# Moving output tiles and two value slots around the turn from self- to cross-attention, and padding the context keys with zeros

## The chip, the cores and the metric

The kernel runs on one core of a Trainium2 chip. The metric is the device time of one execution in microseconds. It is given as the median of several executions. One more execution was taken with the profiler, and all durations of single instructions come from that one.

## What is computed

The reference is one transformer block in float32 on `x` of shape 2 x 1024 x 256 and a context of shape 2 x 154 x 192. There are 16 heads of 64 channels.

```python
h = layernorm(x, ln1);  x = attention(h, h, sa_w*) + x        # 1024 keys
h = layernorm(x, ln2);  x = attention(h, context, ca_w*) + x  # 154 keys
h = layernorm(x, ln3);  p = h @ ff_w1 + ff_b1
a, gate = split(p);     x = (a * gelu(gate)) @ ff_w2 + ff_b2 + x

# attention: softmax(q k^T / 8) v for each head, joined, @ wo + bo
```

## The kernel before

Two heads make a pair, so each of the two batch entries has 8 pairs. A pair of one batch entry is a unit, and there are 16 units in self-attention and again 16 in cross-attention. The order of the instructions on every engine is the order in which the program emits them: the schedule is written by hand, in loops over slots, and tile pools add the waits.

**Self-attention** runs in 128 slots, 8 to a unit. A slot takes two groups of 64 query rows. TensorE makes the scores (L379), DVE takes the maximum of each row (L539), ACT the exponentials with their sums (L390). The keys of one query row lie in two halves on different partitions, so a small DMA on the SP queue exchanges the row statistics `st` (L400). A slot later `join` (L404 to L417) makes the common scale: on POOL `dd` (L408 to L410), on ACT `ee` (L412), on POOL `zz` and `den` (L414, L416). DVE takes the reciprocal `rd` (L486) and POOL multiplies the probabilities by it (L490, four instructions in a slot). Two slots after its scores a group is transposed by DVE into `pT` (L504). When the four slots of a half unit are transposed, two value slots multiply them with the values on TensorE (`self_values`, `weigh`, L426) and ACT copies the sums to `oT` (L524).

In the slots that have no values of their own, `run_work` fills TensorE from lists. `work` holds the projections of the next unit, `outs` the output tiles (L357: four matmuls for one tile of 128 rows; DVE adds the result to `x`, L364), and `side` the pieces of a normalization. `later` holds work that is issued one piece in each slot, among it the bias additions on POOL (L259) and DMAs. The result of a piece is copied out of PSUM in the slot after, by `flush(stores)` or `flush(adds)`. Pieces from `run_work` share two PSUM banks (`mm_tile`), scores share two tiles of two banks each (`ps_s`), and value sums have two banks (`sum_tile`). A piece can start only when the bank of the piece but one before it has been copied out.

**Cross-attention** runs in 48 slots, three to a unit. A slot makes the scores of three, three or two query tiles (L654), DVE the maximum `neg` (L659), ACT the exponentials (L670), POOL scales by the reciprocals one slot later (L681), and DVE transposes two slots later into a ring (`pT_ca`, L697). SP's DMAs regroup blocks of the ring into the tile `wf` (L714), and four or more slots later `cross_values` (L730) uses them. The context values `v_ca` have 154 rows: two copies of ACT bring the first 128 of them to their place (L627), one the last 26 (L628). The last block of 128 x 256 is first set to zero by POOL (L613), and DMAs then spread its rows over the partitions (L630, L635).

The tile `wf` also holds the weights of the feed-forward part, which are loaded from `hold_gated` on, two DMAs in a slot. It takes the buffer of the last self-attention `pT`, so it has to wait for the last value slot.

**The turn between the two** is where the change lies. The last unit has slots 120 to 127 (`p`), and cross slots are counted from 0 (`c`). In the last unit before the change, slots 120, 121, 124 and 125 run one piece each: the two query projections of the first cross unit, its keys, its values. The last four output tiles of the first half of batch entry 1 (tiles 4 to 7) enter `outs` in cross slot 0. The last two value slots run in cross slots 2 and 3, inside `self_drain`, that is ahead of the projections that `run_work` puts into these slots.

Of the kernel before, what the change touches and what calls it, by code (L numbers as in the profile page):

```python
# [8 lines left out]
F32 = mybir.dt.float32  # L9
# [4 lines left out]
P = 128  # L14
# [4 lines left out]
def tile_transformer_block(ctx: ExitStack, tc: tile.TileContext, a: dict, out: bass.AP):  # L19
    nc = tc.nc  # L20
# [3 lines left out]
    B, S, D = x.shape  # L24
# [6 lines left out]
    NT = S // P  # L31
# [7 lines left out]
    VC = 2 * P  # L39
    HB = 512  # L40
    QG = 2 * KB
    NM = P // QG
    QH = S // 2
    GH = QH // QG
# [104 lines left out]
    ident = const.tile([P, P], F32, tag="ident", name="ident")  # L149
    make_identity(nc, ident)  # L150

    ctxT = const.tile([CC, 2, B * T], F32, tag="ctxT", name="ctxT")

    def turn_rows():
        pt = spare["bank"]("p_rows")
# [5 lines left out]
    def turn_context(b):  # L161
        pc = spare["bank"](f"pc{b}")
        for c in range(2):
            for i in range(2):
                nc.tensor.transpose(
                    pc[:CC, c * T + i * KP:c * T + (i + 1) * KP],
                    cn[b][:, i, c * CC:(c + 1) * CC], ident[:KP, :KP],
                )
        return lambda: nc.scalar.copy(
            ctxT[:, :, b * T:(b + 1) * T], pc[:CC, :2 * T].rearrange("p (c k) -> p c k", c=2)  # L170
        )

    hT, vs, qk, oT = {}, {}, {}, {}
# [265 lines left out]
    def run(piece):  # L439
        done = piece()  # L440
        if done is not None:
            (adds if getattr(done, "adds", False) else stores).append(done)
# [109 lines left out]
    def self_beside(ui):  # L552

        if ui + 2 >= NU:
            load_pair("ca", ui + 2 - NU)
        elif ui > 0:
            load_pair("sa", units[ui + 2][1])
        nxt = self_pieces(*units[ui + 1]) if ui + 1 < NU else cross_pieces(*units[0])
        if ui + 1 < NU:
            work.extend(nxt)  # L560
        else:

            work.extend(nxt[:2])
            held.extend(nxt[2:])
        if HP <= ui < NU - 2:
            ob, oh = divmod((ui - HP) // HP, 2)
            t0 = (ui % HP) * 2
            out_pieces("sa", ob, oh, (t0, t0 + 1))
        if ui == 1:
            norm_beside("sa", 1)  # L570
        if ui == NPAIR + HP:
            norm_beside("ca", 0)

    def self_drain(p):

        late = scale_groups(*joins.pop(0)) if joins else None
        if p - LAG < SA:
            turn_groups(p - LAG)
        if late:
            late()  # L580
        h, hg = divmod(p, SH)
        if hg >= LAG and h - 1 < 2 * NU:
            run(lambda: self_values(h - 1, hg - LAG))


    CG = [(t, min(TG, NT - t)) for t in range(0, NT, TG)]
# [3 lines left out]
    def cross_pieces(b, pr):  # L590

        t = {}

        def q(n):
            if n == 0:
                t["q"] = p2.tile([P, S], F32, tag="QT", name=f"q_ca{b}_{pr}")
                t["k"] = p2.tile([P, S], F32, tag="KT", name=f"k_ca{b}_{pr}")
                qk["ca", b, pr] = (t["q"], t["k"])
            return project_half(t["q"], f"q_ca{b}_{pr}", wsl["ca", pr, "q"], hT["ca", b], n, scale)

        def keys():
            pk = mm_tile(f"pk_ca{b}_{pr}")
            for c in range(2):
                nc.tensor.matmul(
                    pk[:, :T], lhsT=wsl["ca", pr, "k"][:, c, :],
                    rhs=ctxT[:, c, b * T:(b + 1) * T], start=(c == 0), stop=(c == 1),
                )
            return lambda: nc.scalar.copy(t["k"][:, :T], pk[:, :T])

        def values():  # L610

            v = vs["ca", b, pr // 2] = pt_.tile([P, NM + 1, VC], F32, tag="V", name=f"v_ca{b}_{pr}")
            nc.gpsimd.memset(v[:, NM, :], 0.0)  # L613
            pv = mm_tile(f"pv_ca{b}_{pr}")
            m = T - P
            for n, rows_ in ((0, P), (1, m)):
                for c in range(2):
                    nc.tensor.matmul(
                        pv[:rows_, n * VC:(n + 1) * VC],
                        lhsT=ctxT[:, c, b * T + n * P:b * T + n * P + rows_],  # L620
                        rhs=wsl["ca", pr, "v"][:, c, :], start=(c == 0), stop=(c == 1),
                    )

            def store():
                for n in range(NM):
                    own = slice(n * QG, (n + 1) * QG)
                    nc.scalar.copy(v[own, n, :], pv[own, :VC])  # L627
                nc.scalar.copy(v[:m, NM, :], pv[:m, VC:])  # L628
                later.insert(0, lambda: [
                    nc.sync.dma_start(  # L630
                        out=v[(1 - n) * QG:(2 - n) * QG, n, :], in_=v[n * QG:(n + 1) * QG, n, :])
                    for n in range(NM)
                ])
                later.insert(1, lambda: [
                    nc.sync.dma_start(out=v[a4 * KB:a4 * KB + m, NM, :], in_=v[:m, NM, :])  # L635
                    for a4 in range(1, P // KB)
                ])

            return store

        return [lambda: q(0), lambda: q(1), keys] + ([values] if pr % 2 == 0 else [])

    def cross_first(c):

        ui, n = divmod(c, len(CG))
        b, pr = units[ui]
        t0, nt = CG[n]
        q, k = qk["ca", b, pr]
        k = k[:, :T]
        sc = ps_s.tile([P, 2, HB], F32, tag="s", name=f"sc_{c}")  # L650
        for i in range(nt):
            for j in range(2):
                r = slice(j * DH, (j + 1) * DH)
                nc.tensor.matmul(  # L654
                    sc[:, j, i * T:(i + 1) * T], lhsT=q[r, (t0 + i) * P:(t0 + i + 1) * P],
                    rhs=k[r, :], start=True, stop=True,
                )
        neg = small.tile([P, 2, TG], F32, tag="neg", name=f"neg_{c}")
        nc.vector.tensor_reduce(  # L659
            neg[:, :, :nt], sc[:, :, :nt * T].rearrange("p j (i k) -> p j i k", k=T), AX.X, ALU.max,  # L660
            negate=True,
        )

        def then():
            pr_ = pp_.tile([P, 2, TG, NB * KB], F32, tag="P", name=f"p_{c}")
            nc.gpsimd.memset(pr_[:, :, :, T:], 0.0)
            den = small.tile([P, 2, TG], F32, tag="den", name=f"den_{c}")
            for j in range(2):
                for i in range(nt):
                    nc.scalar.activation(  # L670
                        pr_[:, j, i, :T], sc[:, j, i * T:(i + 1) * T], AF.Exp,
                        bias=neg[:, j, i:i + 1], accum_out=den[:, j, i:i + 1],
                    )

            def late():

                rden = small.tile([P, 2, TG], F32, tag="rden", name=f"rden_{c}")
                nc.vector.reciprocal(rden[:, :, :nt], den[:, :, :nt])  # L678
                for j in range(2):
                    for i in range(nt):  # L680
                        nc.gpsimd.tensor_scalar(  # L681
                            pr_[:, j, i, :T], pr_[:, j, i, :T], rden[:, j, i:i + 1], 1.0,
                            op0=ALU.mult, op1=ALU.mult,
                        )
                crossed[c] = pr_

            return late

        return then
# [172 lines left out]
    with tc.manual_schedule():  # L862
# [45 lines left out]
        for p in range(SA):  # L908
            if p % (2 * SH) == 0:
                self_beside(p // (2 * SH))  # L910
            if p == SA - SH:
                work.extend(held)
                held.clear()
            then = self_first(p)
            flush(stores)
            late = then()
            if p >= LAG:
                turn_groups(p - LAG)
            flush(adds)
            if late:  # L920
                late()
            if later:
                later.pop(0)()
            h, hg = divmod(p, SH)
            if h == 0 or hg < LAG:

                full = hg % 2 == 0 or outs and p < SA - 2 * SH
                run_work(2 if full and p < SA - 2 * SH else 1, 1, sum_tile)
            else:
                run(lambda: self_values(h - 1, hg - LAG))  # L930

        for c in range(CA):
            if c == 0:
# [1 line left out]
                    [P, 2 * NK, QH // 2], F32, tag="pT", name="pT_ca"  # L935
                ).rearrange("p a b -> p (a b)")[:, :3 * 2 * NB * NT * KB].rearrange(
                    "p (u n j q) -> p u n j q", u=3, n=NB, j=2)
            if c == 0:
                out_pieces("sa", B - 1, 0, range(NT // 2, NT))
            if c == SH + 1:  # L940
                out_pieces("sa", B - 1, 1, range(NT))
                outs.append(lambda: load_out("ca"))
            if c == SH:
                w1, w2 = hold_gated()
            if c % len(CG) == 0:
                cross_beside(c // len(CG))
# [12 lines left out]
            cross_weigh(c)  # L959
            flush(stores)  # L960
            run_work(2, 1, n_sum=2 * (SH < c < 2 * NPAIR and c % len(CG) == 0))
            for _ in range(min(2, len(later))):
                later.pop(0)()

# [58 lines left out]
```

## Time and profile before

| | us |
|---|---|
| median of 3 runs | 1173.76 (1172.14 to 1174.32) |
| profiled execution, its own time | 1171.99 |
| span of the profiled execution | 1170.1 |
| TensorE busy | 1142.5 |
| DVE busy | 830.1 |
| POOL busy | 667.5 |
| ACT busy | 644.1 |

The span goes from the first to the last instruction. The profile names every group by its line, its engine and the tiles it writes and reads. "Idle before" is the time that the engine stood still just ahead of an instruction, with the instruction that ended the wait. `PEld` are weight loads, which overlap with matmuls. Each float32 matmul of the program appears as two records. `po` is a value slot, `s` the self scores, `sc` the cross scores, `pq`, `pk` and `pv` projections, `py` an output tile, `poc` the cross values.

Self-attention takes the time to 729.5 us, cross-attention the time to about 1000 us, and the feed-forward part the rest.

### The profile page before, as it was taken

What the parts mean: (1) busy time and instruction counts of PE and PEld (TensorE: products, weight loads), DVE (VectorE), ACT (ScalarE), POOL (GpSimd) and SP (SyncE); (2) the same over time, 40 slices, a digit from 0 to 9 for tenths busy, and PEclk for the clock granted to TensorE, in tenths of its full rate; (3) what the DMA queues carried; (4) which work ended last, traced back from release to release, by engine and by line L of the source; (5) the groups of instructions that cost most, each with busy time, mean ns of one, the idle gap of its engine ahead of it and who ended that gap; (6) DMA issues with size and microseconds to landing.
All of it is one profiled execution on the core that took longest, in us unless ns stands there. A gap on an engine that the chain in (4) does not pass through costs nothing.

```text
span 1170.1 us, 31736 instructions
## 1 busy us (share of the span) xinstructions
PE 1142.5 (98%) x11931; PEld 672.0 (57%) x11931; DVE 830.1 (71%) x1170; ACT 644.1 (55%) x2055; POOL 667.5 (57%) x1563
## 2 busy tenths in 40 slices
PE   9999999999999999999999998999999999999998
PEld 6434444545545545545545443665556567888887
DVE  4888998898888898898989887547555664232222
ACT  5656676665666666566666755447655572041111
POOL 1778777877767777777777787436644453030000
PEclk9999999999999999999999998999999999999999
DMA  2411011101101101101101100166444433000000
GB/s 82 109 26 34 12 25 34 21 21 34 21 16 34 21 16 34 21 16 34 21 16 21 27 20 7 52 167 157 111 103 99 102 80 73 1 19 10 18 10 18
DMA packets 87018, 51.06 MB, mean 44 GB/s; under 512 B 30742, under 2 KB 77650, under 8 KB 86866
## 3 DMA queue, kind: packets, MB, share of 16 engines
q1 hardware_dynamic: 83650, 46.42, 17.6%
q10 hardware_dynamic: 3216, 2.62, 0.7%
q8 instruction: 94, 1.54, 0.5%
q14 instruction: 58, 0.48, 0.1%
HBM read 19.52 MB, written 2.10 MB: 18 GB/s over the span
## 4 chain that ended last, share of the span: by engine, by line
PE 78%; ACT 7%; POOL 6%; DVE 3%; issue 3%; DMA 2%; SPq 1%; DVEq 0%; ACTq 0%; POOLq 0%
PE po L426 15%; PE s L379 15%; PE pa L818 9%; PE py_sa L357 5%; PE py_ca L357 5%; PE pf L841 5%; ACT p L390 4%; PE pq_ca L296 4%; PE poc L730 4%; PE pv_sa L312 4%; PE pk_sa L296 3%; POOL p L490 3%; PE pq_sa L296 3%; PE sc L654 3%; DMA st<-st 2%
## 5 line engine op out<-in xcount | busy, mean ns | idle before, releaser
L390 ACT ACTIVATE p<-s,st 128x512 f32<-128x512 f32 x512 | 345.1, 686 | 218.7 <-DVE st L539 207.8
L490 POOL TENSOR_SCALAR p<-p,rd,ee 128x512 f32<-128x512 f32 x512 | 385.6, 767 | 43.9 <-DVE rd L486 43.3
L539 DVE TENSOR_REDUCE st<-s 128x2 f32<-128x1024 f32 x256 | 301.4, 1219 | 44.8 <-PE s L379 36.9
L504 DVE STREAM_TRANSPOSE pT<-p 128x1024 f32<-128x1024 f32 x256 | 302.4, 1219 | 0.5 <-POOL p L490 0.4
L379 PE MATMUL s<-k_sa,q_sa 64*32 64x512 f32 x4096 | 256.7, 601 | 19.1 <-ACT p L390 18.0
L426 PE MATMUL po<-pT,v_sa 64*64 64x256 f32 x4096 | 236.1, 380 | 1.2 <-DVE pT L504 1.2
L426 PEld LDWEIGHTS po<-pT,v_sa 64*64 64x64 f32 x4096 | 150.8, 133 | 110.4 <-issue 39.4
L681 POOL TENSOR_SCALAR p<-p,rden 128x154 f32<-128x154 f32 x256 | 96.8, 398 | 119.8 <-DVE rden L678 118.6
L379 PEld LDWEIGHTS s<-k_sa,q_sa 64*32 64x32 f32 x4096 | 59.6, 106 | 151.5 <-ACT p L390 64.2
L670 ACT ACTIVATE p<-sc,neg 128x154 f32<-128x154 f32 x256 | 96.0, 394 | 88.6 <-DVE rden L678 84.4
L818 PE MATMUL pa<-hT_ln,wf 128*128 128x256 f32 x512 | 121.0, 379 | 0.0
L827 DVE SCALAR_TENSOR_TENSOR u<-pa,cols,gate 128x256 f32<-128x256 f32 x64 | 31.0, 484 | 124.1 <-ACT gate L824 124.1
L824 ACT ACTIVATE gate<-pa,cols 128x256 f32<-128x256 f32 x64 | 30.3, 474 | 152.1 <-PE pa L818 152.1
L818 PEld LDWEIGHTS pa<-hT_ln,wf 128*128 128x128 f32 x512 | 96.8, 190 | 13.7 <-issue 0.8
L390 ACT ACTIVATION_READ_ACCUMULATOR p<-s,st 128x1 f32 x512 | 103.6, 202 | 0.0
L659 DVE TENSOR_REDUCE neg<-sc 128x6 f32<-128x924 f32 (+1 forms) x48 | 48.6, 1013 | 48.4 <-PE sc L654 48.4
L414 POOL TENSOR_TENSOR zz<-ee,st 128x8 f32<-128x8 f32 x128 | 25.9, 202 | 81.6 <-ACT ee L412 81.6
L312 PEld LDWEIGHTS pv_sa<-sa_wv,hT_ln 128*128 128x128 f32 x512 | 59.3, 192 | 16.3 <-issue 13.8
L841 PE MATMUL pf<-wf,u 128*128 128x256 f32 x256 | 65.0, 379 | 0.2 <-DVE u L827 0.2
L312 PE MATMUL pv_sa<-sa_wv,hT_ln 128*128 128x128 f32 x512 | 62.4, 278 | 0.0
L296 PE MATMUL pk_sa<-hT_ln,sa_wk 128*128 128x512 f32 (+1 forms) x132 | 60.8, 596 | 0.2 <-ACT q_sa L305 0.2
L357 PE MATMUL py_ca<-ca_wo,o_ca 128*128 128x256 f32 x256 | 60.8, 384 | 0.3 <-ACT hT_ln L238 0.3
(73 smaller groups left out, 1230.1 us busy)
## 6 DMA issues: line engine op xcount, KB each, us to landing
wf<-pT_ca SPq DMA_DIRECT2D x128, 128.0 KB
st<-st SPq DMA_DIRECT2D x512, 1.0 KB
v_sa<-v_sa SPq DMA_DIRECT2D x64, 128.0 KB
wf<-in_L_xattn_ff_w_dram SPq DMA_DIRECT2D x12, 256.0 KB
sa_wq<-in_L_xattn_sa_wq_dram SPq DMA_DIRECT2D x16, 128.0 KB
sa_wk<-in_L_xattn_sa_wk_dram SPq DMA_DIRECT2D x16, 128.0 KB
sa_wv<-in_L_xattn_sa_wv_dram SPq DMA_DIRECT2D x16, 128.0 KB
ca_wq<-in_L_xattn_ca_wq_dram SPq DMA_DIRECT2D x16, 128.0 KB
```

The costliest lines, as they stand in the source:

```text
L296: nc.tensor.matmul(pq[:, own], lhsT=wt[:, c, :], rhs=h[:, c, n * HB + own.start:n * HB + own.stop], start=(c == 0), stop=(c == NC - 1),)
L312: nc.tensor.matmul(pv[:, i * P:(i + 1) * P], lhsT=h[:, c, (n * GT + i) * P:(n * GT + i + 1) * P], rhs=wt[:, c, :], start=(c == 0), stop=(c ...
L357: nc.tensor.matmul(py[:, :D], lhsT=o[:, i, t * P:(t + 1) * P], rhs=wo[kind][:, half * HP + i, :], start=(i == 0), stop=(i == HP - 1),)
L379: nc.tensor.matmul(sc[a4 * KB:(a4 + 1) * KB, j, :], lhsT=q[r, c:c + KB], rhs=k[r, h * HB:(h + 1) * HB], start=True, stop=True, tile_positi ...
L390: nc.scalar.activation(pr[:, j, :], sc[:, j, :], AF.Exp, bias=st[:, 0, 0, i, j:j + 1], accum_out=st[:, 0, 1, i, j:j + 1],)
L426: nc.tensor.matmul(po[a2][j * DH:(j + 1) * DH, :QH // 2], lhsT=v[r, t, e, j * DH:(j + 1) * DH], rhs=pT[r, j * NK + n, :], start=(t == 0 an ...
L490: nc.gpsimd.tensor_scalar(pr[:, j, :], pr[:, j, :], rd[:, c:c + 1], ee[:, 0, c:c + 1], op0=ALU.mult, op1=ALU.mult,)
L504: nc.vector.transpose(halves[h][:, :, c:c + KB], groups.pop(0).rearrange("p j (n k) -> p (j n) k", k=KB))
L539: nc.vector.tensor_reduce(st[:, 0, 0, i, :], sc[i], AX.X, ALU.max, negate=True)
L681: nc.gpsimd.tensor_scalar(pr_[:, j, i, :T], pr_[:, j, i, :T], rden[:, j, i:i + 1], 1.0, op0=ALU.mult, op1=ALU.mult,)
L818: nc.tensor.matmul(pa[:, half, :TF * P], lhsT=w1[:, c, half * DF + f * P:half * DF + (f + 1) * P], rhs=h[:, c, t0 * P:(t0 + TF) * P], star ...
L841: nc.tensor.matmul(sums[blk][i][:, :D], lhsT=sums[blk, "u"][:, f, i * P:(i + 1) * P], rhs=w2[:, f, :], start=(f == 0), stop=(f == NF - 1),)
```

## The change

- In the last unit of self-attention, slots 120, 121, 124 and 125 run two pieces each instead of one. The four output tiles that were queued in cross slot 0 are put into the lists of this unit: two behind the query projections, two behind keys and context values.
- The last two value slots move from cross slots 2 and 3 to cross slots 3 and 4, and in each slot behind `run_work`. `hold_gated` moves from cross slot 4 to cross slot 5 with them.
- The transposed context `ctxT` is padded from 154 to 160 columns for each batch entry and set to zero once, at the start, on POOL. The last block of context values is then made from 32 rows, six of them zero, and the eight memsets of `v_ca` are gone.
- The tile `neg` takes the shape 128 x 2 x 4 and shares the buffers of `zz`.

```diff
-    ctxT = const.tile([CC, 2, B * T], F32, tag="ctxT", name="ctxT")
+    ctxT = const.tile([CC, 2, B * TP], F32, tag="ctxT", name="ctxT")
+    nc.gpsimd.memset(ctxT, 0.0)
...
-            work.extend(nxt[:2])
-            held.extend(nxt[2:])
+            spare["out"] = mm_tile
+            last = [lambda t=t: out_piece("sa", B - 1, 0, t) for t in range(NT // 2, NT)]
+            work.extend(nxt[:2] + last[:2])
+            held.extend(nxt[2:] + last[2:])
...
-        h, hg = divmod(p, SH)
-        if hg >= LAG and h - 1 < 2 * NU:
-            run(lambda: self_values(h - 1, hg - LAG))
...
-            nc.gpsimd.memset(v[:, NM, :], 0.0)
-            m = T - P
-            for n, rows_ in ((0, P), (1, m)):
+            for n, rows_ in ((0, P), (1, KB)):
...
-                nc.scalar.copy(v[:m, NM, :], pv[:m, VC:])
+                nc.scalar.copy(v[:KB, NM, :], pv[:KB, VC:])
...
-        neg = small.tile([P, 2, TG], F32, tag="neg", name=f"neg_{c}")
+        neg = small.tile([P, 2, 4], F32, tag="zz", name=f"neg_{c}")
...
-                full = hg % 2 == 0 or outs and p < SA - 2 * SH
-                run_work(2 if full and p < SA - 2 * SH else 1, 1, sum_tile)
+                full = hg % 2 == 0 or outs or p >= SA - 2 * SH
+                run_work(2 if full else 1, 1, sum_tile)
...
-            if c == 0:
-                out_pieces("sa", B - 1, 0, range(NT // 2, NT))
...
-            if c == SH:
+            if c == SH + 1:
                 w1, w2 = hold_gated()
...
             run_work(2, 1, n_sum=2 * (SH < c < 2 * NPAIR and c % len(CG) == 0))
+            if SH - LAG < c <= SH:
+                run(lambda: self_values(2 * NU - 1, c - SH + LAG - 1))
```

More of the change, by code (lines that the diff above doesn't have):

```diff
@@ L41, in tile_transformer_block @@
     QG = 2 * KB
+    TP = NB * KB
     NM = P // QG
@@ L169, in turn_context @@
         return lambda: nc.scalar.copy(
-            ctxT[:, :, b * T:(b + 1) * T], pc[:CC, :2 * T].rearrange("p (c k) -> p c k", c=2)
+            ctxT[:, :, b * TP:b * TP + T], pc[:CC, :2 * T].rearrange("p (c k) -> p c k", c=2)
         )
@@ L605, in keys @@
                     pk[:, :T], lhsT=wsl["ca", pr, "k"][:, c, :],
-                    rhs=ctxT[:, c, b * T:(b + 1) * T], start=(c == 0), stop=(c == 1),
+                    rhs=ctxT[:, c, b * TP:b * TP + T], start=(c == 0), stop=(c == 1),
                 )
@@ L619, in values @@
                         pv[:rows_, n * VC:(n + 1) * VC],
-                        lhsT=ctxT[:, c, b * T + n * P:b * T + n * P + rows_],
+                        lhsT=ctxT[:, c, b * TP + n * P:b * TP + n * P + rows_],
                         rhs=wsl["ca", pr, "v"][:, c, :], start=(c == 0), stop=(c == 1),
@@ L634, in store @@
                 later.insert(1, lambda: [
-                    nc.sync.dma_start(out=v[a4 * KB:a4 * KB + m, NM, :], in_=v[:m, NM, :])
+                    nc.sync.dma_start(out=v[a4 * KB:(a4 + 1) * KB, NM, :], in_=v[:KB, NM, :])
                     for a4 in range(1, P // KB)
```

## The prediction

> **What bounds the kernel now.** I read the page first, then busy time by stretch around the place of the change, then the order of time of TensorE, ACT and POOL there, and last the chain of waits of the first 20 us.
>
> ```profile
> span 1170.1 us, 31736 instructions
> ...
> PE 1142.5 (98%) x11931; PEld 672.0 (57%) x11931; DVE 830.1 (71%) x1170; ACT 644.1 (55%) x2055; POOL 667.5 (57%) x1563
> ...
> PEclk9999999999999999999999998999999999999999
> ```
>
> TensorE is the bound, and the change removes no work from it. It can win only time in which TensorE waits, or runs slowly: the one 8 in the clock row covers 702 to 731 us, the last unit of self-attention.
>
> ```profile
> 682.43:706.13 23.70, 21.85 (x304) 8.63 (x300) 20.38 (x23) 14.24 (x43) 19.73 (x44) 1.00 0.06 12
> 706.13:712.50 6.37, 4.08 (x34) 1.17 (x35) 5.70 (x7) 3.27 (x11) 5.56 (x12) 0.74 0.04 5
> ...
> 719.95:726.20 6.25, 3.87 (x41) 0.89 (x44) 3.08 (x5) 3.47 (x11) 3.18 (x10) 0.73 0.02 3
> ...
> 739.48:758.41 18.93, 18.93 (x189) 13.11 (x189) 7.25 (x15) 6.87 (x30) 5.83 (x19) 1.00 0.09 30
> ```
>
> Columns: length, then busy time of PE, PEld, DVE, ACT, POOL, then the granted clock. Two stretches of 6 us have TensorE a third idle and at three quarters of its clock; from 739.48 on it never waits.
>
> ```profile
> 705.34 0.79 PE L604 MATMUL pk_ca<-ctxT,ca_wk 96*128 96x154 f32 x4
> 708.42 3.30 PE L379 MATMUL s<-k_sa,q_sa 64*32 64x512 f32 x32 [2.29 <-ACT p L390]
> 711.65 2.53 PE L618 MATMUL pv_ca<-ca_wv,ctxT 96*128 96x256 f32 x8
> ...
> 716.27 3.68 PE L426 MATMUL po<-pT,v_sa 64*64 64x256 f32 x64
> 722.33 3.31 PE L379 MATMUL s<-k_sa,q_sa 64*32 64x512 f32 x32 [2.38 <-ACT p L390]
> ...
> 739.48 3.68 PE L426 MATMUL po<-pT,v_sa 64*64 64x256 f32 x64 [1.17 <-DVE pT L504]
> ```
>
> A slot's 32 score rows take 1.95 us elsewhere; after the idle 2.29 and 2.38 us they take 3.30. The first wait comes because slot 124 gives TensorE only the keys, while a slot's POOL loop is 5.48 us long (scaling starts at 700.16, 705.64, 711.12, 716.60). The second has another cause:
>
> ```profile
> 716.60 3.01 POOL L490 TENSOR_SCALAR p<-p,rd,ee 128x512 f32<-128x512 f32 x4 [0.32 <-DVE rd L486]
> 719.57 0.72 POOL L259 TENSOR_TENSOR x<-x,ca_bo 128x256 f32<-128x256 f32 x1
> 720.24 0.31 POOL L613 MEMSET v_ca<- 128x256 f32 x1
> ...
> 720.58 0.36 ACT L628 COPY v_ca<-pv_ca 26x256 f32<-26x256 f32 x1 [4.22 <-POOL v_ca L613]
> ```
>
> The third v_ca copy waits for a memset queued on POOL behind slot 126's scaling. Behind that copy on ACT stand slot 126's exponentials. Slot 125's scaling starts at 724.58, 7.98 us after slot 124's.
>
> [...]
>
> **The change part by part.** Full-clock paces, start to start on TensorE: a slot's self scores 1.88 us, a value slot 3.61, two q projections 3.63, keys 0.62, context values 2.04, an output tile 1.82, cross scores 0.99 or 0.72 (two tiles).
>
> From 682.43 (slot 120) to 729.46 (cross slot 0) the work is 8 x 1.88 + 4 x 3.61 + 3.63 + 0.62 + 2.04 = 35.77 us and took 47.03: 11.26 lost. From 729.46 to 758.41 (scores of cross slot 5) it is 4 x 0.99 + 0.72 + 2 x 0.62 + 4 x 1.82 + 2 x 3.61 + 2 x 3.63 = 27.68 and took 28.95: 1.27 lost. The edit keeps the same pieces up to cross slot 5: 63.45 us of work, 12.53 lost. So I reckon what is lost afterwards.
>
> Fuller slots: slot 120 takes both q projections, 121 two output tiles, 124 keys and context values, 125 two tiles. Slots then take 5.51, 5.52, 5.49, 5.49, 4.54, 5.52, 5.49, 5.49: cross slot 0 starts at about 725.5 if nothing waits. The other engines: DVE gets two adds (0.39 each) ahead of the reciprocal in slots 122 and 126, where it idled 0.54 per slot, so POOL's loop slips 0.2. POOL's last bias add moves from slot 125 to 127, so slots 124 and 125 have a loop of 4.75. Slot 125's scaling starts at 722.5 (behind reciprocal and adds on DVE), slot 126's at 727.6 (its ee stands behind slot 127's exponentials on ACT). The exponentials of slot 127 start at 723.75, and the first bank is free at 725.1: cross slot 0 does not wait. The two extra copies on ACT (0.6 each) go in its idle 1.6 to 2.2 us per slot; beyond it they would hold exponentials one to one.
>
> No memset: ACT's 4.22 us stall goes; it is inside the 11.26. The seven later memsets (7 x 0.31 = 2.2 us if POOL were the bound) lie on a POOL that idles up to 6.7 us between cross slots, under a TensorE that never waits there: nothing. The copy and DMAs with 32 instead of 26 rows: nothing, same instructions, first used in cross slot 7. On SP these DMAs (2 and 3 issues, 1.2 and 2.5 us) move a slot forward and now stand ahead of slot 126's and slot 127's exchanges of st. From last exponential to dd an exchange took 4.6 us (723.4 to 728.04); from 720.8 and 726.5 it gives 725.4 and 731.1, and POOL comes for them at 725.5 and 731.35: nothing, but with little to spare; what is late there goes into ee one to one.
>
> Emptied cross slots: tiles no longer fill cross slots 1 and 2. The keys of slot 1 need a bank whose copy stands on ACT behind ee of slot 127, and that behind POOL: scaling 727.6 to 730.6, the moved bias add 0.7, memset 0.1, dd 0.6, so ee at 732.0, copy done at 732.8. TensorE has reached this at 725.5 + 0.99 + 3.63 + 0.99 = 731.1: **1.8 us wait**. Then keys and scores to 734.2. Cross slot 3's scores need the bank of slot 1: its max reduce stands on DVE behind the reciprocal of slot 127 (732.9), 1.1, then six exponentials on ACT, 2.2, so free at 736.4: **2.2 us wait**. Then q projections to 741.1. The value slot comes now; its last transpose ends at 737.3 (scaling 733.1 to 736.1, plus 1.25), so the old 1.17 us wait is covered by the projections. Scores, keys, second value slot: cross slot 5 at 682.43 + 63.45 + 4.0 = 749.9, against 758.41.
>
> The clock: [...] A half-clock window costs 0 (it doesn't come, or falls on the wait) to 1.7 (3.4 of work); I take 0.9.
>
> DMAs: the pair regroup of cross slot 5 may start once the last value slot frees the buffer, at 749.9 instead of 758.1, and its first user (cross slot 7) comes 13.9 us later, before 14.05: no wait shown there now. The FFN loads move a slot later, behind this regroup. Unit 2's weights are issued at about 729 and used at 737.4; issued at 733.8 in the trace, their traffic was over by 738.
>
> The memset of ctxT (96x640) sits on POOL ahead of ident:
>
> ```profile
> 1.03 0.30 POOL ident masks.py:199
> 1.33 0.04 issue
> 1.38 5.94 PE warm L877 x32
> 7.32 0.56 PE ph_ln L225 x4
> ```
>
> This chain runs on to the first scores, so the delay stays. 128x128 took 0.20 us and 128x256 0.31, 0.87 ns an element, so 640 take 0.64 (an estimate). [...] Bounds 0 to 0.64; [...] I take +0.5.
>
> The neg tag: a reduce to 2x3 instead of 6 contiguous elements and a shared ring whose readers are done slots before: nothing.
>
> Sum: -12.53 + 4.0 + 0.9 + 0.5 = -7.1. Profiled execution 1171.99 (span 1170.1 and 1.89 around it) becomes 1164.9; the median of the runs shown is 1.77 above that execution: 1173.76 - 7.1 = **1166.7**.
>
> **Rivals.** (B) The POOL loop gets no earlier, because the DVE adds and ACT copies give back what the memset cost. For it: DVE has only 0.54 us spare per slot. Against: ACT's 4.22 us stall is gone for certain. The last transpose then stays at 739.3, with scores already waiting: 739.5 + 3.63 + 3.61 + 0.99 + 0.62 + 3.61 = 752.0, gain 6.4, less 0.5 at the start and 1.7 clock: 1169.6. (C) No wait in cross slots 1 to 3 (exponentials earlier than reckoned): -12.5 + 0.5, 1161.8; against it, ee is tied to POOL. (D) Slower: the first regroup lands late. All must go between the last value slot and cross slot 7, and FFN loads now follow directly on it. TensorE would stand there for the landing time less 13.9 us; it decides from about 21 us on, and at 24 us the time is 1176.8. Against: the same transfer, followed by the same two loads, lands within 14 us now.
> That the change doesn't do what it says is out: the built order has these moves.
>
> **How the numbers follow.** Forecast 0.70 (own range 1164.3 to 1168.7: clock cost 0 to 1.7, start 0 to 0.64, waits 1.2 us off), B 0.17, C 0.06, D and other losses 0.05, no change 0.02. The range 1163.8 to 1170.6 holds the forecast and most of B. Faster by over 0.2% (2.3 us; smaller is not told from no change): 0.92; same 0.03; slower 0.05.
>
> **What would show it.** Right: no 3.30 us score rows in the last unit, cross slot 0 at about 726 us, no ACT wait on v_ca, two TensorE waits of about 2 us in cross slots 1 to 3 (keys behind the q copies, scores behind exponentials), warm matmuls starting at 2.0. Wrong: score waits remaining in slots 121 to 127, the first poc waiting for a DMA, or value slots waiting on transposes.

## The result and the profile after

The changed kernel takes 1166.70 us (median of 6 executions, 1165.68 to 1167.64) against 1173.06 us for the kernel before (6 executions, 1172.14 to 1174.32). The ratio is 0.9946 with a 95% interval of 0.9933 to 0.9959: 6.4 us, or 0.54%, faster. Forecast were 1166.7 us and a gain of 7.1 us against the 1173.76 shown then. The profiled execution took 1166.33 us, its span 1164.5: against 1170.1 the span gained 5.6 us. That the median lands on the forecast to a tenth is luck: terms of the sum were wrong in opposite directions, and three more runs of the kernel before moved its own median down by 0.7, as much as the gain fell short.

The page of the changed kernel:

```profile
span 1164.5 us, 31710 instructions
...
PE 1141.3 (98%) x11931; PEld 673.2 (58%) x11931; DVE 828.9 (71%) x1170; ACT 643.3 (55%) x2055; POOL 665.8 (57%) x1556
...
PEclk9999999999999999999999999899999999999999
```

TensorE is busy for almost as long as before (1141.3 us against 1142.5), and the low digit of the clock row has moved one slice to the right. Busy time by stretch of the changed kernel, columns as before:

```profile
682.74:725.76 43.02, 43.02 (x568) 22.00 (x565) 38.91 (x45) 26.58 (x81) 35.89 (x78) 1.00 0.06 12
...
732.40:736.24 3.84, 1.52 (x13) 1.12 (x13) 2.98 (x5) 2.94 (x14) 3.52 (x7) 0.93 0.28 83
736.24:743.89 7.65, 7.65 (x21) 3.76 (x21) 4.89 (x9) 4.41 (x21) 5.69 (x18) 0.59 0.00 1
```

The whole last unit of self-attention, 43.02 us from slot 120 to cross slot 0, has no wait and a clock of 1.00. The loss has moved into cross slots 1 to 3, as the order of time on TensorE shows:

```profile
730.38 1.06 PE L653 MATMUL sc<-k_ca,q_ca 64*128 64x154 f32 x12
732.40 0.79 PE L605 MATMUL pk_ca<-ctxT,ca_wk 96*128 96x154 f32 x4 [0.97 <-ACT q_ca L307]
733.12 0.79 PE L653 MATMUL sc<-k_ca,q_ca 64*128 64x154 f32 x8
736.24 1.91 PE L653 MATMUL sc<-k_ca,q_ca 64*128 64x154 f32 x12 [2.32 <-ACT k_ca L609]
738.08 5.88 PE L298 MATMUL pq_ca<-hT_ln,ca_wq 128*128 128x512 f32 x8
743.89 3.69 PE L428 MATMUL po<-pT,v_sa 64*64 64x256 f32 x64
...
752.82 0.80 PE L653 MATMUL sc<-k_ca,q_ca 64*128 64x154 f32 x8
```

The keys wait for the copy of the q projection, the scores of cross slot 3 for ACT: for the six exponentials that free their bank, which end at 736.01, and for the copy of the keys that stands just behind these on ACT and ends at 736.18. The scores use these keys, so this wait has two feeders that end 0.17 us apart. Scores and projections after the second wait are slow: 1.84 and 5.81 us from start to start at a mean clock of 0.59, against 0.99 and 3.63 at a clock of 1.00. Cross slot 5 starts at 752.82 instead of 758.41. These 5.59 us are the whole gain of the span; behind it TensorE works on as before.

### The profile page after: what moved, and what is told of

Read it like the earlier page. It is cut to its first block, busy times and chain, and to the rows that moved or that the text cites. A ratio compares the mean times of both kernels' runs of the same rounds, so it can differ in the third digit from the quotient of the medians.

```text
span 1164.5 us, 31710 instructions
## 1 busy us (share of the span) xinstructions
PE 1141.3 (98%) x11931; PEld 673.2 (58%) x11931; DVE 828.9 (71%) x1170; ACT 643.3 (55%) x2055; POOL 665.8 (57%) x1556
## 4 chain that ended last, share of the span: by engine, by line
PE 82%; ACT 6%; POOL 3%; DVE 3%; DMA 2%; issue 2%; SPq 1%; DVEq 0%; ACTq 0%; POOLq 0%
PE po L428 16%; PE s L381 16%; PE pa L817 10%; PE py_sa L359 5%; PE py_ca L359 5%; PE pq_ca L298 5%; PE pf L840 5%; PE poc L729 4%; ACT p L392 4%; PE pv_sa L314 4%; PE pk_sa L298 3%; PE sc L653 3%; PE pq_sa L298 3%; DMA st<-st 2%; DVE st L541 2%
## 5 line engine op out<-in xcount | busy, mean ns | idle before, releaser
L381 PE MATMUL s<-k_sa,q_sa 64*32 64x512 f32 x4096 | 253.4, 596 | 12.5 <-ACT p L392 11.2
L298 PE MATMUL pq_ca<-hT_ln,ca_wq 128*128 128x512 f32 x128 | 61.9, 625 | 0.5 <-ACT hT_ln L240 0.5
```

What stands on the lines that cost most here:

```text
L298: nc.tensor.matmul(pq[:, own], lhsT=wt[:, c, :], rhs=h[:, c, n * HB + own.start:n * HB + own.stop], start=(c == 0), stop=(c == NC - 1),)
L381: nc.tensor.matmul(sc[a4 * KB:(a4 + 1) * KB, j, :], lhsT=q[r, c:c + KB], rhs=k[r, h * HB:(h + 1) * HB], start=True, stop=True, tile_positi ...
```

## Experiments

Each profile starts its first scores a little earlier or later (17.4 to 18.5 us), so I read every trace from slot 120's scores to those of cross slot 5. Between them lies the same work in every kernel, 63.45 us at a clock of 1.00. The kernel before needs 75.98 us there and the changed one 70.08. What a kernel needs beyond 63.45 us is lost, to waits or to a reduced clock. Times are ratios to the kernel before on the same chip; the first four kernels ran on one chip, the next four on another and the last three together.

### The parts alone

The zero padding without the rest (the shared `neg` buffers come with it), then the tiles, then the value slots:

```diff
+    nc.gpsimd.memset(ctxT, 0.0)
...
-            nc.gpsimd.memset(v[:, NM, :], 0.0)
```

> The kernel before with the zero-padded context keys alone (no memset of v_ca; neg shares the buffers of zz). Theory 'waits' (the memset cost not its own 0.31 us but ACT's queue: 4.22 us of stall, then a TensorE wait at slower clock in slot 127): ACT's wait on v_ca is gone, slot 127's scores take 1.95 us with no wait, cross slot 0 comes at about 725.7 instead of 729.5, but the value slot still waits for its last transpose at about 736.3, so the span falls by about 3.0 us (2.2 to 3.6), the 0.2 us at the start taken off. Rival 'chain' (POOL's scaling loop alone sets when the last transpose ends, and the memset is 0.31 us of it): 0 to -0.6 us.

Measured: ratio 0.9979 (0.9970 to 0.9987), which is 2.5 us of 1173.05; the interval is 1.5 to 3.5. On TensorE from slot 120 to cross slot 5 it takes 73.16 us. The memset itself is 0.31 us, so it was the queue behind it that cost: the theory of waits holds. The value slot still waits for its last transpose, as expected:

```profile
737.57 3.69 PE L428 MATMUL po<-pT,v_sa 64*64 64x256 f32 x64 [1.53 <-DVE pT L506]
```

```diff
-            work.extend(nxt[:2])
-            held.extend(nxt[2:])
...
+            work.extend(nxt[:2] + last[:2])
+            held.extend(nxt[2:] + last[2:])
...
-            if c == 0:
-                out_pieces("sa", B - 1, 0, range(NT // 2, NT))
```

> The kernel before with the four output tiles moved into slots 121 and 125 alone; the memset of v_ca and the place of the value slots stay. Theory 'waits': the context values are now made in slot 124, so their memset stalls ACT one slot earlier, ahead of slot 125's exponentials, and TensorE waits about 2.3 us ahead of slot 126's scores. The first 3.30 us row is gone. In cross slot 2 the value slot waits about 3 us for its transpose with nothing left to fill. Span -3.5 us (-2.5 to -5.5). Rival 'sum' (moving tiles gives back all the time in which slots 121 to 125 waited, 7 us and more, whatever else is done): -6 us or more.

Measured: ratio 0.9990 (0.9982 to 0.9998), 1.2 us with an interval of 0.2 to 2.1. Both theories missed. TensorE in this kernel:

```profile
716.49 3.67 PE L357 MATMUL py_sa<-sa_wo,o_sa 128*128 128x256 f32 x8 [2.74 <-ACT v_ca L630]
...
741.83 6.32 PE L426 MATMUL po<-pT,v_sa 64*64 64x256 f32 x64 [3.26 <-DVE pT L504]
```

And ACT:

```profile
716.07 0.36 ACT L630 COPY v_ca<-pv_ca 26x256 f32<-26x256 f32 x1 [4.04 <-POOL v_ca L615]
```

The stall of ACT is there again, a slot earlier, and I had overlooked who needs that copy: not only the exponentials behind it, but also the second tile of slot 125, whose bank it frees. The tile stands 2.74 us for it and then runs at reduced clock (3.59 us from start to start for 1.82; the mean clock from 682 to 760 us is 0.93). In the last unit the tiles still fill much: cross slot 0 comes 47.91 us after slot 120 (47.03 before) with 7.28 us more of work ahead of it. But the cross slots that they leave lose 6.5 us up to cross slot 5, where the kernel before lost 1.3: the value slot waits 3.26 us and runs at reduced clock (6.32 us for 3.68). So nearly all that the tiles win in the last unit is lost again behind it, and the 2.74 us are due to the memset, which holds the PSUM bank that the tiles need; the reduced clock came behind that wait.

```diff
-        if hg >= LAG and h - 1 < 2 * NU:
-            run(lambda: self_values(h - 1, hg - LAG))
...
+            if SH - LAG < c <= SH:
+                run(lambda: self_values(2 * NU - 1, c - SH + LAG - 1))
```

> The kernel before with the last two value slots a slot later and behind their slots' projections alone. Theory 'waits': only the 1.17 us wait of the value slot for its last transpose is covered, the rest stays as before: -1.2 us (0 to -1.3). Rival 'sum' (it is worth the wait of about 3 us that it would cover once the tiles are gone): -3 us.

Measured: ratio 0.9996 (0.9988 to 1.0004), 0.5 us with an interval of -0.5 to 1.4. The 3 us of the rival are excluded; the 1.2 us expected lie inside the interval, and so does nothing at all. In the trace (here `hold_gated` moves along, as in the changed kernel) the value slot has no wait left, but cross slots 1 and 2 have new ones of 0.18 and 0.60 us.

The parts alone add up to some 4 us, together they give 6.4; with intervals of about 1 us on each part, the times alone do not show the difference. The traces do, one execution each: from slot 120 to cross slot 5 the padding takes off 2.8 us, the tiles 1.1, and both together 5.7 (the next kernel). Padding and tiles help each other. What the tiles alone have in addition in the last unit is the wait for the bank and the reduced clock behind it, 4.9 us lost there; with the padding beside them nothing is lost there (43.08 us to cross slot 0, at a clock of 1.00). The profiles of the padding alone and of the value slots alone happened to lose no clock (1.00 from 682 to 760 us in both), so they gain more in their traces (2.8 and 1.1 us) than by their times (2.5 and 0.5).

### The changed kernel without the move of the value slots

```diff
+        h, hg = divmod(p, SH)
+        if hg >= LAG and h - 1 < 2 * NU:
+            run(lambda: self_values(h - 1, hg - LAG))
...
-            if SH - LAG < c <= SH:
-                run(lambda: self_values(2 * NU - 1, c - SH + LAG - 1))
```

> The changed kernel with its value slots left where they were, in cross slots 2 and 3 ahead of the projections. Theory 'waits': TensorE stands in cross slot 2 for the last transpose (end 737.0) instead of standing in cross slot 3 for a bank (736.2), so the move of the value slots is worth only about 0.8 us here: span 0.8 us above the changed kernel (0 to 1.8), some 4.8 us below the kernel before. Rival 'sum' (the move of the value slots covers the whole wait of some 3 us): 2.5 to 4 us above the changed kernel.

Measured: ratio 0.9955 (0.9942 to 0.9967), 1.0 us above the 0.9946 of the changed kernel, with intervals that overlap. From slot 120 to cross slot 5 it is 70.32 us against 70.08. TensorE in that kernel:

```profile
737.94 5.93 PE L428 MATMUL po<-pT,v_sa 64*64 64x256 f32 x64 [3.27 <-DVE pT L506]
```

The wait is 3.27 us for the transpose instead of 2.32 us for the bank, and the clock falls there as well: 0.73 from 732 to 740 us and 0.84 from 740 to 748, the same two means as in the changed kernel. So in the traces the move of the value slots covers only the difference of two waits that end almost together, 0.2 us, as the theory of waits has it. By the times it is worth 1.0 us with an interval of about 2 us either way, which by itself would not exclude the lower end of the rival's 2.5 to 4.

### The clock behind the waits

```diff
+            if c in (1, 2):
+                fill = sum_tile(f"fill{c}")
+                for _ in range(8 if c == 1 else 20):
+                    nc.tensor.transpose(fill[:, :P], ident, ident)
             run_work(2, 1, n_sum=...)
```

> The changed kernel with 8 transposes of the identity ahead of the keys in cross slot 1 and 20 behind the scores of cross slot 2, into a free bank that nobody reads: they add no result, only activity where TensorE waits. Theory 'clock' (the scores of cross slot 3 and the q projections behind them, 1.84 and 5.81 us instead of 0.99 and 3.63, are slow because the waits of 1.0 and 2.4 us halved the clock): they fall to 0.99 and 3.63, span -3.0 us (-2.4 to -3.2). Rival 'traffic' (they are slow because other engines or DMAs share the memory there, or the waits themselves are the whole cost): 0, or up to +0.5 where the transposes end after the bank is free.

TensorE with the filling transposes:

```profile
735.32 2.40 PE L961 MATMUL fill<-ident 128*128 128x128 f32 x20
737.72 1.06 PE L653 MATMUL sc<-k_ca,q_ca 64*128 64x154 f32 x12
738.70 3.70 PE L298 MATMUL pq_ca<-hT_ln,ca_wq 128*128 128x512 f32 x8
```

Scores and projections are back at 0.98 and 3.63 us from start to start, with the clock at 1.00 throughout, and cross slot 5 comes 67.67 us after slot 120, 2.4 us less than in the changed kernel. The rival falls: the rows were slow because of the clock, not because of traffic. In time the kernel has a ratio of 0.9933 (0.9919 to 0.9946), 1.5 us below that of the changed kernel, with intervals that overlap; the 3.0 us expected are not reached in the trace either, because the last unit took 0.3 us longer than in the changed kernel's profile (43.35 against 43.02) and the keys, behind ee, came another 0.3 us later.

How much the clock takes differs between executions of one kernel. In the first profile of the changed kernel it stands at half for 6.7 us:

```profile
735.80:742.50 6.70, 6.26 (x17) 3.38 (x18) 5.33 (x9) 4.45 (x24) 6.13 (x19) 0.50 0.00 1
```

In the profile of the same kernel that was taken later (below), the projections take 4.40 us from start to start instead of 5.81, so that scores and projections lose 1.6 us instead of 3.0 (the mean clock from 735 to 745 us is 0.83 instead of 0.66):

```profile
736.19 1.91 PE L653 MATMUL sc<-k_ca,q_ca 64*128 64x154 f32 x12 [2.33 <-ACT k_ca L609]
738.03 4.47 PE L298 MATMUL pq_ca<-hT_ln,ca_wq 128*128 128x512 f32 x8
```

And the padding alone has a wait of 2.31 us at the place where the kernel before waits 2.29, without any loss of clock (1.00 from 706 to 714 us). Here is TensorE with the padding alone, first scores behind that wait, where a group of 16 takes the usual 1.09 us:

```profile
709.58 1.09 PE L381 MATMUL s<-k_sa,q_sa 64*32 64x512 f32 x16 [2.31 <-ACT p L392]
```

### What holds the two waits

```diff
-            if later:
+            if later and p < SA - 1:
                 later.pop(0)()
```

> The changed kernel with POOL's last bias add one slot later, behind the scaling of slot 127, so that it no longer stands ahead of that slot's dd. Theory 'ee chain' (keys of cross slot 1 wait for a bank whose copy stands on ACT behind ee, which waits for POOL, and the max of cross slot 1 stands behind the reciprocal of the same chain): ee, reciprocal and both waits move by 0.72 us, span -0.7 us with the clock as it is, up to -3 us if the thinner waits keep the clock up. Rival 'TensorE side' (the keys wait for the q projections themselves or their copies, not for POOL): 0.

Measured: ratio 0.9940 (0.9927 to 0.9952), and the two waits are 1.01 and 2.33 us, as in the changed kernel (0.97 and 2.32). POOL with the later bias add:

```profile
731.24 0.13 POOL L665 MEMSET p<- 128x36 f32 x1
731.99 0.20 POOL L410 TENSOR_TENSOR dd<-st 128x4 f32<-128x4 f32 x1 [0.62 <-DMA st<-st]
```

The bias add no longer stands ahead of dd, but dd now waits 0.62 us for the exchange of st by DMA. So the chain through ee has two feeders that end within 0.1 us of each other (0.72 us of bias add gave way to 0.62 us of wait), and taking one away shows the other. The unchanged waits are what the rival forecast, but the trace speaks for the chain: ACT's ee waits 1.17 us for dd, the copies of q stand straight behind ee, and the keys wait for the first of them. My theory named the right chain and only one of its two feeders.

```diff
-            last = [lambda t=t: out_piece("sa", B - 1, 0, t) for t in range(NT // 2, NT)]
+            last = [lambda t=t: out_piece("sa", B - 1, 0, t) for t in range(NT // 2, NT - 1)]
...
+            if c == 2:
+                out_pieces("sa", B - 1, 0, [NT - 1])
```

> The changed kernel with one of the four output tiles put back, into cross slot 2, where TensorE waits 2.4 us. Theory 'clock': slot 126's scores wait about 1.2 us for a bank, but cross slot 0 comes no later (about 725.1 to 725.8), the tile fills 1.8 of the 2.4 us, the clock stays full: span -3.6 us against the changed kernel (-2.5 to -4.5). Rival 'full slots' (every tile taken from the last unit of self-attention costs its 1.8 us there, and the cross slots' waits stay): 0 to +2 us.

Measured: ratio 0.9929 (0.9917 to 0.9942). Cross slot 0 comes 43.36 us after slot 120 (43.02), so the tile taken out of slot 125 costs 0.3 us there; the clock stays at 1.00, and cross slot 5 comes at 68.24 us. This is 1.8 us less than in the changed kernel, not the 3.6 that I expected: the keys wait 1.45 us (dd waits 0.54 us for the exchange of st, although the bias add is in its old place), and a new wait of 1.15 us stands ahead of slot 126's scores, as reckoned. Of the 4.8 us lost none is clock; the changed kernel lost 6.6, of which 3.0 were clock. So the tile removed the loss of clock, and what is lost to waits is not less but 1.2 us more.

With tile, bias add and the memset of ctxT moved behind the start:

```diff
-    nc.gpsimd.memset(ctxT, 0.0)
...
         emit(k1)
+        nc.gpsimd.memset(ctxT, 0.0)
```

> The changed kernel with one output tile in cross slot 2, the last bias add a slot later, and the memset of ctxT on POOL behind the four rstd of the start instead of ahead of the identity. If the three are what is left: first scores at 17.4 instead of 17.65, keys' wait about 0.3 us, no wait ahead of cross slot 3, clock full: span -4.5 us against the changed kernel (-3.5 to -5.2), some 10 us below the kernel before. If the gains don't add: no better than the better of the two others.

Measured: ratio 0.9936 (0.9923 to 0.9948), 68.29 us from slot 120 to cross slot 5: no better than the tile alone. The exchange of st takes the place of the bias add once more (dd waits 1.07 us), and the second q projection of cross slot 3 waits 0.58 us for the bank of the tile. First scores came at 17.82, inside the scatter of all kernels.

### Side by side

The changed kernel, the one tile in cross slot 2, and two tiles put back into banks that are free (the edit of the last):

```diff
-            last = [lambda t=t: out_piece("sa", B - 1, 0, t) for t in range(NT // 2, NT)]
-            work.extend(nxt[:2] + last[:2])
-            held.extend(nxt[2:] + last[2:])
+            last = [lambda t=t: out_piece("sa", B - 1, 0, t) for t in range(NT // 2, NT - 2)]
+            work.extend(nxt[:2] + last[:1])
+            held.extend(nxt[2:] + last[1:])
...
+            if c in (1, 2):
+                spare["out"] = sum_tile
+                run(lambda: out_piece("sa", B - 1, 0, NT - 3 + c))
             run_work(2, 1, n_sum=...)
```

> The changed kernel again, for a comparison on one chip with the next two: as before, 6 to 7 us below the kernel before. From slot 120's scores to cross slot 5's 70.1 us where the clock halves behind the waits of cross slots 1 and 2, about 67.1 where it doesn't.

> The kernel with one output tile put back into cross slot 2, again, beside the changed kernel: from slot 120's scores to cross slot 5's 68.2 us, full clock, time 1.8 us below the changed kernel (0.5 to 2.5). Rival: what was seen on another chip was scatter between executions, 0.

> The changed kernel with two of the four tiles put back, one into cross slot 1 ahead of the keys and one into cross slot 2, both into the banks of the value sums, which are free there. Theory 'clock and waits': slots 125 and 126 wait 1.2 and 1.8 us instead, cross slot 0 comes no later (43.0 to 43.4 us after slot 120), the keys' wait is filled, cross slot 5 at 67.5 us after slot 120: 2.5 us below the changed kernel (1.5 to 3). Rival 'full slots' (tiles taken out of slots 121 and 125 cost there what they save later): 0 or slower.

| kernel | median us | ratio to before | slot 120 to cross slot 5, us |
|---|---|---|---|
| before | 1172.92 | 1 | |
| changed | 1166.54 | 0.9946 (0.9933 to 0.9960) | 68.97 |
| one tile in cross slot 2 | 1164.67 | 0.9930 (0.9918 to 0.9943) | 67.51 |
| two tiles, value banks | 1165.01 | 0.9933 (0.9921 to 0.9946) | 67.47 |

The changed kernel repeats its ratio. With one tile put back the kernel is 1.9 us faster by the medians, and its five executions (1164.58 to 1165.72) scarcely touch those of the changed kernel (1165.67 to 1167.67), although the intervals of the two ratios overlap. In the two profiles the changed kernel loses 5.5 us against 63.45, 1.6 of them to the clock, and the kernel with one tile 4.1, none of them to the clock (1.00 from slot 120 to cross slot 5). So again it is the clock that the tile wins, and the waits keep their length; the transposes that compute nothing came to the same 67.67 us. Two tiles come out the same as one: the keys' wait is gone,

```profile
734.01 1.99 PE L359 MATMUL py_sa<-sa_wo,o_sa 128*128 128x256 f32 x8
735.84 0.69 PE L605 MATMUL pk_ca<-ctxT,ca_wk 96*128 96x154 f32 x4
```

but slots 122, 125 and 126 wait 2.7 us in all, so the sum is what it was. The changed kernel with one tile put back is about 8.3 us below the kernel before, and by its ratio it came out below the changed kernel both times.

## Why the prediction was right, and where it was not

**The fuller slots.** Right. Reckoned were 43.05 us from slot 120 to cross slot 0, without a wait; measured are 43.02. POOL's scalings of slots 125, 126 and 127 start at 722.40, 727.20 and 732.74, against 722.5, 727.6 and 733.1, though slot 120 came 0.31 us later. (The scaling at 716.60 ahead of the memset, which the prediction calls slot 126's, runs in slot 126 but belongs to slot 124.)

**The memset.** Right: ACT's wait on v_ca is gone, as its order of time after the change shows,

```profile
710.65 0.74 ACT L626 COPY v_ca<-pv_ca 64x256 f32<-64x256 f32 x2
711.40 0.36 ACT L627 COPY v_ca<-pv_ca 32x256 f32<-32x256 f32 x1
```

and the padding alone gave 2.5 us for 0.31 us of work. What the prediction did not see is that the tiles need the same copy: without the padding they are worth 1.2 us.

**Emptied cross slots.** The two waits came at the places named, for the banks named, the second for the copy of the keys besides. The first was reckoned at 1.8 us (its own times, 731.1 to 732.8, give 1.7) and was about 1.0: counted from slot 120, POOL's chain ran up to 0.7 us ahead of the reckoning. The second was reckoned at 2.2 and was 2.4 (733.84 to 736.24). Their sum was 3.4 instead of 4.0.

**The clock.** The term that was mis-sized: "A half-clock window costs 0 […] to 1.7 […]; I take 0.9". The 0.9 was my estimate; measured were 3.0 in the first profile and 1.6 in the second. The upper bound assumed one stretch of 3.4 us at half clock. The profile of the kernel before has two of that length, both at 0.50: from 709.13 to 712.54 us, behind the wait of 2.29 us, and from 722.76 to 726.17, behind that of 2.38. The first of them, in a row that begins 0.13 us before it and ends 0.14 us before its end, so that the mean is 0.52:

```profile
709.00:712.40 3.40, 3.40 (x34) 0.88 (x19) 2.73 (x5) 1.10 (x5) 2.59 (x8) 0.52 0.05 8
```

In the first profile of the changed kernel the clock stood at 0.50 for twice that, 6.83 us from 735.67 to 742.50. It fell there 0.57 us before the second wait ended; from the end of the first wait to the end of the second (732.40 to 736.24) TensorE was busy for 1.52 of 3.84 us.

**The start.** The term that was wrong: "+0.5" for the memset of ctxT, my estimate between its bounds. The estimate of its length was right (0.64, measured 0.63), but the delay did not stay. The order of time on TensorE and the chain of waits after the change read:

```profile
1.91 5.31 PE L876 MATMUL warm<-ident 128*128 128x128 f32 x32 [1.91 <-POOL ident masks.py:199]
```

```profile
0.72 3.38 DMA x<-in_x_dram
```

The warm matmuls start 0.53 us later (1.91 instead of 1.38) but take 5.31 us instead of 5.94, so they end no later than before (7.22 against 7.32; the clock reads 1.00 over the first 17.4 us of both kernels), and the chain goes from the load of x through DVE, POOL and ACT to the transposes. First scores came 0.24 us later, as much as the load of x ended later (first statistics at 4.12 instead of 3.88): from the first statistics it is 13.53 us to the first scores in both kernels. So the memset cost nothing in these two profiles. In five other profiles with it (the experiments up to the first run of the one tile) first scores came at 17.81 to 18.48 us, in two without it (the value slots alone, the tiles alone) at 17.91 and 17.93, and with it behind the start at 17.82. Whether it had a part in these differences is not shown.

**The sum.** Reckoned against the profiled executions was -7.1, measured -5.7 (1171.99 to 1166.33). From slot 120 to cross slot 5 the clock took 2.1 us more than allowed for and the waits 0.6 less; the keys of cross slots 1 and 4 took 0.1 us more each than the pace they were reckoned at. Up to slot 120 the delay was 0.31 us, 0.2 less than the 0.5 put in. Together this is the 1.5 us by which the span fell short (5.6 for 7.1). (The prediction's own range, 1164.3 to 1168.7, is 0.1 to 0.2 us narrower at each end than its three bounds added up.)

**The rivals.** B fell: the last transpose ended at 737.04 against 739.33 before, because POOL's loop did get earlier. C fell by the two waits. D fell: from cross slot 5 on TensorE waits for no DMA, and its first cross values start at 766.57, 13.75 us after the buffer was free. The range 1163.8 to 1170.6 held the time, and "faster" was right.

## What to carry to other kernels

A small instruction is priced by what stands behind it: 0.31 us of memset on POOL held a copy on ACT, the copy held exponentials and a PSUM bank, and the bank held the work that was meant to fill the gap. Work that is moved to fill one gap leaves another: the last unit lost 11.3 us before and none after, the stretch from cross slot 0 to cross slot 5 1.3 before and 6.7 after. Count the clock beside the waits: in one profile here the two waits took 3.4 us and the half clock behind them a further 3.0; with the one tile in cross slot 2 the waits together stayed as long as they were, the clock was 1.00, and the time was a further 1.9 us lower. Before an instruction is moved off a chain, look for the second feeder that ends at the same time: here it was a DMA only 0.1 us apart.

## What the runs showed that was not expected

Waits of nearly equal length came with a halved clock in one execution and not in another. In the profile of the kernel before, 2.29 us did (0.50 for 3.41 us); with the padding alone 2.31 us at the same place did not, nor did 2.31 and 2.39 us with the value slots alone (1.00 from 682 to 760 us in both). In two profiles of the changed kernel the same waits of 1.0 and 2.3 us cost 3.0 and 1.6 us of clock (0.66 and 0.83 from 735 to 745 us). What decides whether the clock falls no run here shows.

How long it stays at half follows a pattern in these profiles, from slot 120 on:

| profile and place | wait ends, us | clock falls, us | at half for, us | read from |
|---|---|---|---|---|
| changed kernel, first profile, cross slot 3 | 736.24 | 735.67 | 6.83 | clock 0.50 |
| changed kernel without the move, value slot | 737.94 | 735.7 | 6.9 | estimate: clock 0.73 from 732 to 740, 0.84 from 740 to 748 |
| tiles alone, value slot | 741.83 | 738.9 to 740.5 | 6.6 to 8.2 | estimate: 6.25 us for 3.61; clock 0.93 from 682 to 760, less the 3.5 us at the bank |
| before, slot 125 | 708.42 | 709.13 | 3.41 | clock 0.50 |
| before, slot 127 | 722.33 | 722.76 | 3.41 | clock 0.50 |
| tiles alone, tile behind the bank | 716.49 | 716.5 | 3.5 | estimate: 3.59 us for 1.82 |
| late bias add, cross slot 3 | 737.31 | 738.0 | 3.3 | estimate: 1.31 and 4.95 us for 0.99 and 3.63; clock 0.98 from 682 to 760 |
| changed kernel, second profile, cross slot 3 | 736.19 | 736.2 | 3.4 | estimate: clock 0.83 from 735 to 745 |

The estimates take the clock to be either 1.00 or 0.50, the two values that it has around the places read directly, and follow from the means and the slowed work in the traces. In three places the clock fell while TensorE still stood, and stayed at half for 6.83 us in the one that is read directly and about as long in the other two. In five places it fell at the end of the wait or up to 0.7 us behind it, and stayed for 3.41 us in the two read directly and 3.3 to 3.5 in the others. So nearly the same wait came with one length of half clock or with twice that. These are eight cases; no run was made to vary the place.
